# A first ternary product from bfloat16 parts, joined matmul runs, and some of a scan's weighted sums on GpSimd

## The chip, the core and the metric

The kernel runs on one core of a Trainium2 chip. The core has a matrix engine (TensorE, PE in the profile, with its weight loads shown as PEld), a vector engine (VectorE, DVE), a scalar engine for activation functions and copies (ScalarE, ACT), a general engine (GpSimd, POOL) and a queue for transfers (SyncE, SP). Operands lie in SBUF, 128 partitions wide; matmuls write to PSUM, which has eight banks of 128 x 512 float32. GpSimd's instructions here all work in SBUF. The metric is the device time of one launch, in microseconds (us), the median of several runs.

## The reference

The model takes 128 batches of 32 tokens with 256 features (4096 rows in all) and sends them through six residual layers in two levels. Cut to what matters:

```
x = x + cross_attention_0(ctx, layernorm(x))          # softmax over 257 context rows, weights wq, wk, wv
x = x + selective_scan(layernorm(x))                  # 512 channels, 16 states, along the 32 tokens
x = x + ternary_mlp(x)                                # 256 -> 1024 -> 256
x = x + focused_linear_attention(layernorm(x), ctx)   # 16 heads
x = x + latent_attention(layernorm(x))                # 16 heads, keys and values through 64 latents
x = x + quantized_mlp(x)                              # 8-bit rows, ternary weights
```

Two of them are touched by the change:

```
# selective scan: gate, x and delta are projections; A = -exp(A_log), c0 = C_mat[0]
def step(h, (x_t, d_t)):
    h = h * exp(A * d_t[..., None]) + (x_t * d_t)[..., None] * B_mat      # 512 x 16
    y_t = h @ c0                                                          # sum over the 16 states
y = y + x * D_vec;  out = (gate * y) @ W_out.T + b_out

# ternary mlp: absmean(W) = sign(W / g) * min(round(|W / g|), 1), with g = mean |W| + 1e-6
h = x @ absmean(W_fc).T
h = layernorm(gelu(h), ln_w, ln_b)
out = h @ absmean(W_proj).T
```

The ternary weights are -1, 0 and 1. The mlp's input is normalised too: the kernel computes each row's mean and reciprocal deviation, takes the mean off the input or off the weights, and multiplies the deviation in as the scale of the gelu.

## The kernel before

Rows are worked on in 32 groups of 128 (four batches of 32 tokens), and the groups in nine blocks of 2, 4, 4, 4, 4, 4, 4, 4 and 2. For each block there are three stages:

- **Context (`c`)**: `context_group` does the first cross attention of one group and, from the same context rows, the keys and values of the later linear attention (`keys`, `keys_values`). Its float32 matmuls `pkey` and `pval` are the largest part of TensorE's work.
- **Scan (`a`)**: `scan_block` works on a whole block at once, 512 columns (256 in the first and the last block). There are four channel blocks of 128 channels, and each has 16 states. For each state ScalarE computes the decay `a`, DVE scans along the tokens (`tensor_tensor_scan`, giving `h`) and DVE adds `h` times the state's weight `w_st` to `acc`, which lies in a bank of PSUM. `acc` begins as the projection `xd` times `d_vec`, written by ScalarE. After the last state `acc` is multiplied by the gate.
- **Layers (`l`)**: `latent_group` does the four other layers of one group: `mlp`, `linear`, `attention` and `quantized_mlp`, and stores the rows.

In `mlp` the rows of x are transposed as they are, while two statistics run beside this; two runs of two float32 matmuls each (k = 0 and 1, 512 columns each) multiply by `w_fc`, from whose rows the mean was taken off in the set-up (`centred(w_fc, 2)`). In `attention` four runs of matmuls follow one another: the query `pqa`, the latents `plat`, the keys `pka` and, further on, the values `pva`, each in a PSUM bank of its own, with ScalarE's copies between them.

No engine is given its instructions in the order of the program. Every call goes through a `Recorder` (so nearly every instruction in the profile has one line, L540), and a planner, `order`, then places them. It has a cost for each instruction (`ns_of`, with `TAIL` and `HOP` for what passes before another engine can go on), a pair of due times for every group of instructions (`DUE`, one pair for each call of `begin`), and a few settings: `PRICE` weighs the engines where an instruction may go to more than one (`copy`, `relu`, `scaled`), `WINDOW` and `SOONER` let a more urgent instruction go first, and `HORIZON` says how far ahead of the front a new buffer may be opened. Matmuls under one `R.together()` are placed as one run, back to back. The order found is fixed on each engine; what waits is then only for data and buffers. Buffers come from rings: `t2` has 15 tiles of 2 KB per partition, `bank` the eight PSUM banks, and `a_ring` three tiles for the decays.

Of the kernel before, what the change touches and what calls it, by code (L numbers as in the profile page):

```python
# [16 lines left out]
P = 128  # L17
# [77 lines left out]
TAIL = {"vector": 75, "scalar": 100, "gpsimd": 25, "tensor": 130, "sync": 0}  # L95
# [171 lines left out]
class Recorder:  # L267
# [8 lines left out]
    def together(self):  # L276

        recorder = self

        class Joined:  # L280
            def __enter__(self):
                recorder.joined = []

            def __exit__(self, *_):
                parts, recorder.joined = recorder.joined, None
                ways = {"tensor": ([c for p in parts for c in p[0]], sum(p[1] for p in parts), False)}
                recorder.add(ways, [r for p in parts for r in p[2]], [w for p in parts for w in p[3]])

        return Joined()

    def copy(self, out, in_):
        self.record({"scalar": ("copy", (out, in_), {}), "vector": ("tensor_copy", (out, in_), {})})

# [12 lines left out]
    def begin(self, stage):  # L306

        self.stage = stage
        self.group += 1
        self.spans[self.group] = DUE[self.group]  # L310

    def record(self, calls):
# [33 lines left out]
        if self.joined is not None:  # L346
            self.joined.append((*ways["tensor"][:2], reads, writes))
            return
# [205 lines left out]
PRICE = {"tensor": 0.0, "vector": 3.195, "scalar": 3.454, "gpsimd": 8.58, "sync": 0.0}  # L554
WINDOW = 31.919
SOONER = -0.015
AHEAD = 0
HORIZON = 0.832
# [3 lines left out]
def perceiver_kernel(ctx: ExitStack, tc: tile.TileContext, t: dict, out: bass.AP):  # L562
# [92 lines left out]
    def t2k(shape, name, dtype=F32):  # L655
        return ring("t2", 15).tile(shape, name, dtype)
# [51 lines left out]
    w_fc = wts.tile([P, 2, HID], F32, name="w_fc")  # L708
# [135 lines left out]
    def late_setup():  # L844
# [52 lines left out]
        centred(w_fc, 2)  # L897
# [142 lines left out]


# [73 lines left out]
    def scan_block(x):  # L1115
        size = len(x)
        tok, batches = size * P, size * GB
# [17 lines left out]
        for ic in range(4):  # L1135

            dl = t2k([P, TOK], "dl")[:, 0:tok]
            R.scalar.activation(
                dl, project(w_in, DI + ic * P), AF.Relu, bias=b_in[:, 4 + ic : 5 + ic]
            )  # L1140
            xd = project(w_in, ic * P)
            acc = bank("acc")[:, 0:tok]
            R.scalar.activation(
                acc, xd, AF.Identity, bias=bd_in[:, ic : ic + 1], scale=d_vec[:, ic : ic + 1]
            )
            R.vector.scalar_tensor_tensor(xd, xd, b_in[:, ic : ic + 1], dl, ALU.add, ALU.mult)
            dv = dl.rearrange("p (b q) -> p b q", q=LQ)
            for s in range(NST):

                a = a_ring[s % NA][:, 0:batches, :]  # L1150
                R.scalar.activation(
                    a[:, :, 1:LQ], dv[:, :, 1:LQ], AF.Exp, scale=a_neg[:, ic, s : s + 1]
                )
                h = t2k([P, TOK], "h")[:, 0:tok]
                R.vector.tensor_tensor_scan(
                    h, a.rearrange("p b q -> p (b q)"), xd, 0.0, ALU.mult, ALU.add
                )
                R.vector.scalar_tensor_tensor(
                    acc, h, w_st[:, ic, s : s + 1], acc, ALU.mult, ALU.add
                )  # L1160
            R.vector.tensor_tensor(yg[ic], acc, yg[ic], ALU.mult)
        for g in range(size):
# [8 lines left out]
    def mlp(xg):  # L1171

        _, r = stats(xg)
        xT = rows_T(xg)
# [3 lines left out]
        for k in range(2):  # L1178
            ph = bank("ph")
            cols = slice(k * 512, (k + 1) * 512)  # L1180
            with R.together():
                accumulate(ph, [(xT[:, dc, :], w_fc[:, dc, cols]) for dc in range(2)])
# [64 lines left out]
    def attention(xg):  # L1247
# [3 lines left out]
        with R.together():  # L1251
            for c in range(2):
# [3 lines left out]
                )  # L1256
        qT = t1k([P, D], "qTa").rearrange("p (c n) -> p c n", c=2)
        R.scalar.copy(qT, pq[:, 0:D].rearrange("p (c n) -> p c n", c=2))

        pl_ = bank("plat")  # L1260
        with R.together():
            accumulate(pl_[0:LAT, 0:P], [(wkd[:, dc], xT[:, dc, :]) for dc in range(2)])
        lat = t1k([P, P], "lat")[0:LAT]
        R.scalar.copy(lat, pl_[0:LAT, 0:P])

        pk = bank("pka")
        with R.together():
            for c in range(2):
                accumulate(pk[:, c * P : (c + 1) * P], [(wupk[:, c * P : (c + 1) * P], lat)])
        kd = t2k([P, 2, GB, 2, LQ], "kd")  # L1270
        for r in range(2):
# [3 lines left out]
                scale=odd[:, r : r + 1],  # L1275
            )
# [25 lines left out]

        vd = vds[turn[0] % NV]
        turn[0] += 1
        pv = bank("pva")
        with R.together():
            for b in range(GB):
                for r in range(4):
                    R.tensor.matmul(
                        pv[r * LQ : (r + 1) * LQ, b * 64 : (b + 1) * 64],  # L1310
                        lat[:, b * LQ : (b + 1) * LQ],
                        wupv.rearrange("p (j h k) -> p h j k", h=4, k=16)[:, r],
                        start=True, stop=True,
                    )
        for r in range(4):
            rows_ = slice(r * LQ, (r + 1) * LQ)
            R.scalar.copy(
                vd[rows_, :, :, r, 0:16],
                pv[rows_, 0 : GB * 64].rearrange("p (b j n) -> p b j n", b=GB, j=4),
            )  # L1320
# [88 lines left out]
    def latent_group(xg, kvc, rows_out):  # L1409
        mlp(xg)  # L1410
        linear(xg, kvc)
        attention(xg)
        quantized_mlp(xg)
# [4 lines left out]
    for i, size in enumerate(BLOCKS):  # L1418
# [12 lines left out]
        scan_block(x)  # L1431
# [8 lines left out]
NV = 2  # L1440
PAIR = 2
# [4 lines left out]
    (-1.0, -0.9), (-0.011, 0.566), (-0.809, -0.789), (-0.212, 0.821), (-0.767, 0.109),  # L1446
    (-0.01, 0.15), (0.299, 1.222), (0.556, 1.717), (1.591, 2.698), (1.87, 3.034), (0.619, 0.719),
    (0.863, 0.989), (1.148, 1.233), (1.17, 1.732), (1.498, 2.663), (2.591, 3.75425),
    (2.699, 3.86225), (2.806, 3.97), (2.915, 4.07825), (1.618, 1.802), (1.854, 2.163),
    (2.11, 2.23), (2.365, 2.485), (2.459, 3.663), (3.593, 4.75425), (3.7, 4.86225),  # L1450
    (3.807, 4.97025), (3.915, 5.07825), (2.571, 2.704), (2.985, 3.032), (3.115, 3.236),
    (3.365, 3.485), (3.5, 4.663), (4.591, 5.75425), (4.699, 5.86225), (4.807, 5.97025),
    (4.915, 6.07825), (3.61, 3.735), (3.864, 3.99), (4.115, 4.235), (4.365, 4.431), (4.5, 5.663),
    (5.591, 6.755), (5.699, 6.86225), (5.807, 6.97025), (5.915, 7.113), (4.615, 4.733),
    (4.866, 5.033), (5.115, 5.235), (5.365, 5.485), (5.5, 6.663), (6.612, 7.776), (6.72, 7.884),
    (6.7, 8.26), (6.921, 8.145), (5.616, 5.733), (5.924, 6.173), (6.117, 6.235), (6.462, 6.482),
    (6.501, 7.654), (7.288, 8.301), (7.441, 8.497), (7.544, 8.812), (7.594, 8.984),
    (6.632, 6.743), (6.921, 6.941), (7.171, 7.295), (7.361, 7.611), (7.495, 8.077),
    (7.815, 9.377), (7.667, 9.18), (7.008, 8.283), (7.34, 8.982), (7.658, 7.783), (7.829, 7.849),
    (8.0, 8.585), (8.023, 9.464), (8.392, 9.052),  # L1460
# [78 lines left out]
```

## Time and profile before

| | |
|---|---|
| median of 3 runs | 1763.43 us (1761.84 to 1765.21) |
| the profiled execution | 1760.93 us |
| its span, first to last instruction | 1759.2 us |
| TensorE (PE) busy | 1660.5 us, 94% |
| VectorE (DVE) busy | 1554.4 us, 88% |
| ScalarE (ACT) busy | 1430.8 us, 81% |
| GpSimd (POOL) busy | 1117.0 us, 63% |
| mean granted TensorE clock | 0.973 of full speed |
| transfers | 59.69 MB, 34 GB/s on average |

A group of instructions is shown as engine, operation, result and operands, shape and count, then the busy time in us and the mean duration of one in ns, and last the time for which the engine was idle just before them and what ended that. A float32 matmul appears as two records. Matmuls overlap in the array, so the mean duration of one is more than what it adds to a row of them; some records of matmuls are missing from the trace. In a line by stretch of time the first figures are the stretch and its length, then the busy time and number of instructions of each engine, the granted clock and the load of the transfers.

### The profile page before, as it was taken

Reading aid. Unit: us, or ns where it says so; the run is one execution under the profiler, and the core shown is the slowest. Engines: PE = TensorE matmul, PEld = TensorE weight load, DVE = VectorE, ACT = ScalarE, POOL = GpSimd, SP = SyncE. Lnnn points to the kernel's source line nnn. Section 1 sums busy time; section 2 is a strip of 40 time slices with the busy share of each in tenths; the row PEclk is TensorE's granted clock in tenths of the full one; section 3 lists DMA queues with packets and bytes.
Section 4 is the critical chain, followed back from the end, with each engine's and each line's share of the span. In section 5 each row is a group of like instructions: output and inputs, shape, how many; then the busy total and the mean of one; then the engine's idle time right before and its main releaser. Section 6 shows DMA issues by size and latency. Waiting matters only on the chain.

```text
span 1759.2 us, 44923 instructions
## 1 busy us (share of the span) xinstructions
PE 1660.5 (94%) x17268; PEld 1211.7 (69%) x17299; DVE 1554.4 (88%) x3083; ACT 1430.8 (81%) x3442; POOL 1117.0 (63%) x1827
## 2 busy tenths in 40 slices
PE   8999999999999999999999999999999989597886
PEld 6787667766776777766776767766776667366564
DVE  3599799999898999899899999979999999999865
ACT  4587888888788997889788888889888898786655
POOL 5675556744776677666776747865776375347476
PEclk9999999999999999999999999999999999798886
DMA  7221101000110011001100021001100000000000
GB/s 243 74 83 47 61 29 32 29 31 4 48 42 2 16 59 35 29 2 40 41 29 29 7 65 37 29 2 40 40 29 29 1 8 20 4 4 5 5 4 22
DMA packets 44758, 59.69 MB, mean 34 GB/s; under 512 B 8704, under 2 KB 27008, under 8 KB 44544
## 3 DMA queue, kind: packets, MB, share of 16 engines
q1 hardware_dynamic: 44544, 56.81, 10.1%
q8 instruction: 137, 2.24, 0.5%
q14 instruction: 77, 0.63, 0.1%
HBM read 52.32 MB, written 4.19 MB: 32 GB/s over the span
## 4 chain that ended last, share of the span: by engine, by line
PE 75%; DVE 12%; ACT 7%; issue 1%; POOL 1%; DMA 0%; SPq 0%; DVEq 0%; ACTq 0%; POOLq 0%
PE pkey L540 13%; PE pval L540 11%; PE pproj L540 9%; PE pT L540 5%; PE pmlp L540 5%; DVE h L540 5%; PE ph L540 4%; PE pk L540 3%; PE pcT L540 3%; PE pout L540 3%; PE pq L540 3%; DVE acc L540 2%; PE psc L540 2%; PE pqa L540 2%; PE po L540 2%; PE pya L540 2%
## 5 line engine op out<-in xcount | busy, mean ns | idle before, releaser
L540 DVE TENSOR_TENSOR_SCAN h<-a,pproj 128x512 f32<-128x512 f32 (+1 forms) x576 | 617.4, 1087 | 12.4 <-ACT a L540 11.6
L540 ACT ACTIVATE a<-dl,a_neg 128x496 f32<-128x496 f32 (+1 forms) x576 | 369.8, 662 | 60.9 <-DVE h L540 57.6
L540 DVE SCALAR_TENSOR_TENSOR acc<-h,w_st,acc 128x512 f32<-128x512 f32 (+1 forms) x576 | 392.4, 681 | 0.1
L540 PE MATMUL pval<-wkv,cT 128*128 128x256 f32 x1024 | 245.7, 385 | 8.8 <-ACT hid L540 2.3
L540 PE MATMUL pkey<-wkv,cT 128*128 128x256 f32 x1024 | 238.1, 386 | 0.0
L540 POOL TENSOR_TENSOR ku<-ku,e 128x512 f32<-128x512 f32 x128 | 162.1, 1276 | 101.1 <-ACT ku L540 93.3
L540 PEld LDWEIGHTS pval<-wkv,cT 128*128 128x128 f32 x1024 | 189.6, 191 | 44.6 <-issue 7.4
L540 ACT ACTIVATE ks<-ku 128x256 f32<-128x256 f32 x512 | 208.1, 412 | 14.3 <-POOL ku L540 13.1
L540 PEld LDWEIGHTS pkey<-wkv,cT 128*128 128x128 f32 x1024 | 189.3, 190 | 37.7 <-issue 14.5
L540 POOL TENSOR_TENSOR ku<-ks,ku 128x512 f32<-128x512 f32 x128 | 163.7, 1285 | 29.8 <-ACT ks L540 29.1
L540 ACT ACT_TABLE_LOAD x114 | 146.3, 1283 | 5.1 <-PE ph L540 2.5
L540 POOL TENSOR_TENSOR kn<-kn,halves 128x4 f32<-128x4 f32 x128 | 134.1, 1048 | 22.5 <-ACT ks L540 21.7
L540 ACT ACTIVATE vf<-pval,kf 128x256 f32<-128x256 f32 x256 | 107.9, 471 | 40.0 <-PE pval L540 24.5
L540 POOL TENSOR_TENSOR rstd<-rstd,halves 128x1 f32<-128x1 f32 x224 | 123.7, 553 | 15.8
L540 POOL TENSOR_SCALAR rstd<-mv 128x1 f32<-128x1 f32 x224 | 42.9, 192 | 133.7 <-DVE mv L540 110.2
L540 PE MATMUL pproj<-xTs,w_in 128*128 128x512 f32 (+1 forms) x288 | 122.4, 552 | 0.5 <-ACT hT L540 0.2
L540 PE MATMUL ph<-w_fc,xT 128*128 128x512 f32 x256 | 120.2, 597 | 0.6 <-ACT xT L540 0.5
L540 PE MATMUL pmlp<-w_pr,hT 128*128 128x256 f32 x512 | 116.7, 381 | 1.5 <-ACT hT L540 1.2
L540 PEld LDWEIGHTS pmlp<-w_pr,hT 128*128 128x128 f32 x512 | 95.8, 190 | 20.7 <-issue 4.8
L540 ACT ACTIVATION_READ_ACCUMULATOR ks<-ku 128x1 f32 x512 | 99.4, 194 | 0.0
L540 ACT COPY cT<-pcT 128x512 f32<-128x512 f32 x128 | 71.8, 595 | 12.2 <-PE pcT L540 11.8
L540 DVE BATCH_NORM_STATS2 st<-x 128x6 f32<-128x256 f32 x192 | 78.7, 413 | 2.9 <-POOL x L540 1.7
(259 smaller groups left out, 3583.1 us busy)
## 6 DMA issues: line engine op xcount, KB each, us to landing
cx<-in_ctx_dram SPq DMA_DIRECT2D x64, 512.0 KB
x<-in_x_dram SPq DMA_DIRECT2D x32, 128.0 KB
cr<-in_ctx_dram SPq DMA_DIRECT2D x128, 32.0 KB
out_dram<-x SPq DMA_DIRECT2D x32, 128.0 KB
vlz<-vl SPq DMA_DIRECT2D x128, 1.1 KB
w_in<-in_w_inT_dram SPq DMA_DIRECT2D x1, 1024.0 KB
raw_fc<-in_w_fcT_dram SPq DMA_DIRECT2D x2, 512.0 KB
raw_pr<-in_w_prT_dram SPq DMA_DIRECT2D x2, 512.0 KB
```

What stands on the lines that cost most here:

```text
L540: ins = getattr(engine, name)(*(traced(a) for a in args), **{k: traced(v) for k, v in kw.items()}).ins
```

## The change

- In `mlp` the mean is now taken off x before the transposition, not off `w_fc`. The transposed rows are split into three bfloat16 parts (a cast, what is left, a cast, what is left), and the run for each half has six bfloat16 matmuls in place of two float32 ones. `w_fc` is stored in bfloat16, which holds -1, 0 and 1 exactly. The casts may go to three engines (`cast`), the subtractions to two (`either`).
- In `attention` the latents are computed in the run of the query, and the values in the run of the keys, in one bank each; the copies into `vd` come before the scores.
- In `scan_block` the first two states (the first four in the last two blocks) are weighted and summed by GpSimd in a tile `some` in SBUF, which starts as the projection times `d_vec`. DVE's first weighting then adds to `some` and writes `acc`, whose bank is opened only there.
- The planner gets other costs, prices and settings; a run is charged 15 or 90 ns more; `t2` has 17 tiles; `part` divides the stages (the contexts in two, the scan by channel block, the layers by layer), so that `DUE` has 251 pairs in place of 78.

```diff
-TAIL = {"vector": 75, "scalar": 100, "gpsimd": 25, "tensor": 130, "sync": 0}
+TAIL = {"vector": 75, "scalar": 90, "gpsimd": 25, "tensor": 215, "sync": 0}
...
+                small = any(p[4] for p in parts)
+                ns = sum(p[1] for p in parts) + (90 if small else 15)
+                ways = {"tensor": ([c for p in parts for c in p[0]], ns, False)}
...
+    def cast(self, out, in_):
+        self.record({
+            "scalar": ("copy", (out, in_), {}), "vector": ("tensor_copy", (out, in_), {}),
+            "gpsimd": ("tensor_copy", (out, in_), {}),
+        })
...
+    def part(self):
         self.group += 1
         self.spans[self.group] = DUE[self.group]
...
-PRICE = {"tensor": 0.0, "vector": 3.195, "scalar": 3.454, "gpsimd": 8.58, "sync": 0.0}
-WINDOW = 31.919
-SOONER = -0.015
-AHEAD = 0
-HORIZON = 0.832
+PRICE = {"tensor": 0.0, "vector": 2.435, "scalar": 0.756, "gpsimd": 0.394, "sync": 0.0}
+WINDOW = 39.422
+SOONER = 0.032
+AHEAD = 0.074
+HORIZON = 1.395
...
-        return ring("t2", 15).tile(shape, name, dtype)
+        return ring("t2", 17).tile(shape, name, dtype)
...
-    w_fc = wts.tile([P, 2, HID], F32, name="w_fc")
+    w_fc = wts.tile([P, 2, HID], BF16, name="w_fc")
...
-        centred(w_fc, 2)
...
+        pooled = LATE_POOLED if late else POOLED
...
-            acc = bank("acc")[:, 0:tok]
+            some = t2k([P, TOK], "some")[:, 0:tok]
             R.scalar.activation(
-                acc, xd, AF.Identity, bias=bd_in[:, ic : ic + 1], scale=d_vec[:, ic : ic + 1]
+                some, xd, AF.Identity, bias=bd_in[:, ic : ic + 1], scale=d_vec[:, ic : ic + 1]
             )
...
-                R.vector.scalar_tensor_tensor(
-                    acc, h, w_st[:, ic, s : s + 1], acc, ALU.mult, ALU.add
-                )
+                weight = w_st[:, ic, s : s + 1]
+                if s < pooled:
+                    R.gpsimd.tensor_scalar(h, h, weight, None, ALU.mult)
+                    R.gpsimd.tensor_tensor(some, some, h, ALU.add)
+                else:
+                    if s == pooled:
+                        acc = bank("acc")[:, 0:tok]
+                    R.vector.scalar_tensor_tensor(
+                        acc, h, weight, some if s == pooled else acc, ALU.mult, ALU.add
+                    )
...
     def mlp(xg):
-
-        _, r = stats(xg)
-        xT = rows_T(xg)
+        mv, r = stats(xg)
+        xc = t1k([P, D], "xc")
+        R.either.tensor_scalar(xc, xg, mv[:, 0:1], None, ALU.subtract)
+        xT = t1k([P, D], "xT")
+        transposed(xc, xT.rearrange("p (c n) -> p c n", c=2), 2)
+
+        x3 = t2k([P, 3, D], "x3", BF16)
+        R.cast(x3[:, 0, :], xT)
+        R.either.tensor_tensor(xT, xT, x3[:, 0, :], ALU.subtract)
+        R.cast(x3[:, 1, :], xT)
+        R.either.tensor_tensor(x3[:, 2, :], xT, x3[:, 1, :], ALU.subtract)
...
-                accumulate(ph, [(xT[:, dc, :], w_fc[:, dc, cols]) for dc in range(2)])
+                accumulate(ph, [
+                    (x3[:, k3, dc * P : (dc + 1) * P], w_fc[:, dc, cols])
+                    for dc in range(2) for k3 in range(3)
+                ])
...
+            accumulate(pq[0:LAT, D : D + P], [(wkd[:, dc], xT[:, dc, :]) for dc in range(2)])
+        lat = t1k([P, P], "lat")[0:LAT]
+        R.scalar.copy(lat, pq[0:LAT, D : D + P])
...
         pk = bank("pka")
+        pv = pk[:, D : 2 * D]
         with R.together():
             for c in range(2):
                 accumulate(pk[:, c * P : (c + 1) * P], [(wupk[:, c * P : (c + 1) * P], lat)])
+            for b in range(GB):
+                for r in range(4):
+                    R.tensor.matmul(
+                        pv[r * LQ : (r + 1) * LQ, b * 64 : (b + 1) * 64],
+                        lat[:, b * LQ : (b + 1) * LQ],
+                        wupv.rearrange("p (j h k) -> p h j k", h=4, k=16)[:, r],
+                        start=True, stop=True,
+                    )
...
-        scan_block(x)
+        scan_block(x, i >= len(BLOCKS) - 2)
...
+POOLED = 2
+LATE_POOLED = 4
```

## The prediction

> **What bounds the kernel now.** The execution that was profiled took 1760.9 us, 1.7 us more than its span of 1759.2 us and 2.5 us less than the median of the runs, 1763.4 us. I sum against the span and add 4.2 us at the end. First I read the busy times by stretch. The cuts are mine: set-up up to 200 us, the regular blocks up to 1400, then up to 1661, where the last scan and its weighting end, and the rest.
>
> ```profile
> core 0: us, PE busy (x) PEld busy (x) DVE busy (x) ACT busy (x) POOL busy (x), PEclk, DMA share, GB/s
> 0.00:200.00 200.00, 188.93 (x1810) 146.19 (x1811) 143.57 (x330) 135.35 (x419) 128.29 (x206) 0.98 0.33 105
> 200.00:1400.00 1200.00, 1177.13 (x12356) 855.34 (x12377) 1102.88 (x2044) 1035.18 (x2475) 781.39 (x1265) 1.00 0.09 30
> 1400.00:1560.00 160.00, 132.11 (x1274) 95.87 (x1276) 155.46 (x290) 131.46 (x284) 81.78 (x142) 0.94 0.03 10
> 1560.00:1661.00 101.00, 86.02 (x1104) 61.94 (x1104) 90.87 (x243) 75.58 (x168) 56.18 (x92) 0.88 0.02 4
> 1661.00:1759.00 98.00, 76.34 (x729) 52.34 (x732) 61.64 (x179) 53.20 (x99) 69.35 (x124) 0.78 0.04 12
> ```
>
> From 200 to 1400 TensorE (PE) is busy 98% and VectorE (DVE) 92%: matmul time decides. From 1400 to 1661 the context matmuls run out (the last `pval` is at 1484 us), PE falls to 84%, and DVE is busy 246.3 of 261 us: the scans of the last two blocks decide. In the last 98 us nothing is full: that is the latency of the last groups' layers, one operation after the other. GpSimd (POOL) has room everywhere. Then the groups of instructions that the change touches, or that are nearest to what it adds:
>
> ```profile
> L540 PE MATMUL ph<-w_fc,xT 128*128 128x512 f32 x256 | 120.2, 597 | 0.6 <-ACT xT L540 0.5 <-DVE hq L540 0.2
> L540 DVE SCALAR_TENSOR_TENSOR acc<-h,w_st,acc 128x512 f32<-128x512 f32 x448 | 332.1, 741 | 0.1
> L540 DVE SCALAR_TENSOR_TENSOR acc<-h,w_st,acc 128x256 f32<-128x256 f32 x128 | 60.5, 472 | 0.0
> L540 POOL TENSOR_TENSOR ku<-ks,ku 128x512 f32<-128x512 f32 x128 | 163.7, 1285 | 29.8 <-ACT ks L540 29.1
> L540 POOL TENSOR_SCALAR hq<-hq,qm 128x1024 f32<-128x1024 f32 x32 | 35.7, 1115 | 14.6 <-DVE qm L540 13.7
> L540 POOL TENSOR_SCALAR q<-xn 128x256 bf16<-128x256 f32 x32 | 12.9, 403 | 34.6 <-DVE xn L540 29.3 <-DVE qm L540 4.3
> L540 POOL TENSOR_TENSOR x<-x,s 128x256 f32<-128x256 f32 x32 | 23.3, 728 | 13.6 <-PE pT L540 9.3 <-DVE st L540 4.2
> ```
>
> The reader sees that a weighting on DVE costs 0.741 us (0.472 for the small blocks), and an addition on POOL 1.28 us (0.73). Mean durations of matmuls overlap, so for them I take starts from the timeline:
>
> ```profile
> 1567.62 1.88 PE L540 MATMUL ph<-w_fc,xT 128*128 128x512 f32 x4
> 1569.34 3.62 PE L540 MATMUL pmlp<-w_pr,hT 128*128 128x256 f32 x16
> ...
> 1685.53 1.03 PE L540 MATMUL phq<-w,qT 128*128 128x512 bf16 x4
> 1686.40 0.38 PE L540 MATMUL pT<-ident,x 128*128 128x128 f32 x2
> ```
>
> A float32 run of `ph` (two products, four records) holds PE for 1.72 us; four bfloat16 products of the same width hold it for 0.87, so 0.2175 each, with a new stationary tile for each.
>
> **The change, part by part.** *The product itself.* A run becomes six bfloat16 matmuls: 6 x 0.2175 = 1.305 us, a gain of 0.415 a run, 26.6 us over 64 runs. Of the 256 records 199 lie between 200 and 1400 us (about 50 runs, 20.6 us), 43 up to 1661 and 16 after it. Only the first 20.6 us shorten a stretch that PE sets; the rest falls where PE has idle time.
>
> *The centring of `w_fc` in the set-up goes.* Two runs like the old `ph`, 3.4 us of PE, and some 3.9 us of DVE. PE is busy 94% of that stretch: 3 us.
>
> *The new work per group* is a centring of x and four operations that split it (cast, rest, cast, rest), on 256 columns. On POOL: 0.47 (403 ns plus one pointer, about 70 ns) + 2 x 0.40 + 2 x 0.73 = 2.73 us, 87 us over 32 groups; on DVE about 0.41 + 2 x 0.35 + 2 x 0.415 = 1.94 us, 62 us. The new prices make POOL and ScalarE (ACT) cheaper against DVE than before, so I give DVE a third, 21 us. ACT, at 81%, can take the casts at 0.37 us. None of it binds before 1661, as POOL and ACT have room and DVE loses more than it gains. In the last stretch it is latency: the transposes now wait for the statistics too (0.42 + 0.18 us) and then for 0.44 + 2 x 0.39 + 2 x 0.57, so 3.0 us with hops left out, less a little on PE: +3 us (0 where the other group of the last block covers it, +6 where both groups pay in series).
>
> *Joined runs.* Four runs per group become two in the first half of attention: `lat` with `q`, `v` with `k`. In the timeline eight records of `pqa` hold PE 0.98 us, or 0.245 a product, and the two products of `plat` 0.58, so a run's edge costs at most 0.09 us: 64 edges, 0 to 5.8 us. The waits before `plat` and `pva` are 1.7 and 1.6 us in all. I take 3 us of 0 to 9. The queue behind a joined run waits longer for its first result, by 0.6 us, which later matmuls of other groups cover.
>
> *The pooled states.* Full width: 6 blocks x 4 channel blocks x 2 states, and 16 in the late block: 64 weightings x 0.741 = 47.4 us less on DVE. Half width: 8 in the first block and 16 in the last, 24 x 0.472 = 11.3. Together 58.7 us, 19.4 of it in the two late blocks, whose scans lie almost wholly between 1400 and 1661. POOL pays a multiplication (between the 256- and 1024-wide rows, 0.62 plus 0.07 for the pointer: 0.69 us) and an addition (1.28): 1.97 us x 64 + 1.20 x 24 = 155 us. At most 1117 + 155 + 87 = 1359 us, 80% of the span: still not the bound. DVE goes to about 1554 - 59 - 4 + 21 = 1512. In the stretch from 1400 to 1661, which DVE sets, I count 19.4 less some 4 for splits: -15 us (bounds -8 with all splits on DVE, -19 with none).
>
> *The shared port.* The trace shows DVE held up by POOL now and then: `xn` takes 405 ns in the median and 1439 at worst. The scans, with one operand in PSUM, run at 1165 to 1221 ns beside a POOL that is two thirds busy:
>
> ```profile
> L540 DVE TENSOR_TENSOR_SCAN h<-a,pproj x71: 1165/1210/1221, 300.4 to 498.5; 128x512 f32<-128x512 f32 x71
> ```
>
> Only 36 of the weightings (the first after the pooled states, which now reads `some` and `h` from SBUF) join the exposed kind; at the mean excess of `xn`, 34 ns, that is 1 us, at its worst 37 us. I take 1, as most DVE time keeps an operand in PSUM.
>
> The Trainium skill speaks against this part: "Perfetto Trace Analysis", section "Optimizing Scalar/DVE Operations", says that GpSimd and DVE share an SBUF read port, so that moving work between those two might not help. By the rule the 15 us of the late stretch would be nothing and the sum 15 us higher. The row of the scans above disagrees with it for operations that read PSUM, and I go by the row.
>
> *The order.* Every priority in the planner changes: 251 due spans in place of 78, so each layer and channel block gets its own, two more `t2` buffers, two PSUM banks fewer per attention, `acc` opened two states later, a longer horizon. No row prices this. The bounds: PE idles 66 us between 200 and 1661 (23 + 28 + 15); all of it saved would be -66, twice as much idle +66. Nearest is the stretch to 1400: DVE has 97 us idle there, and 39 more once 58.7 - 19.4 us of weightings are gone, while the late stretch is full of DVE work. Scans of the last blocks brought forward into a seventh of that room of 136 us give -20. I take -20, towards a gain because in both long stretches one engine is near full while another has room.
>
> **Sum.** 1759.2 - 20.6 - 3 - 3 - 15 + 3 + 1 - 20 = 1701.6; with 4.2 us, 1706 us.
>
> **The rivals.** *Smaller gain: the order brings nothing.* Without its -20 the time is 1726. For it: PE is 98% busy to 1400, and the last 98 us are latency that no order shortens. Against it: 136 us of DVE room before 1400. *Larger gain:* the order uses half of the 66 us of PE idle and a third of DVE's room, -50 in place of -20: 1676. For it: the last stretch, where DVE has 36 us free and PE 22, could take work of the groups before, so that the last scan ends sooner. Against it: such work must be ready, and the end stays a chain. *Slower: DVE waits for POOL.* In each channel block the first weighting on DVE waits for all pooled additions. Uncovered, that is 3.9 us for two states less the 1.2 of the second scan, and a POOL queue in order, whose head may wait too:
>
> ```profile
> POOL rstd L540 <- DVE mv L540: 110.2, 57, 11.4
> POOL ku L540 <- ACT ku L540: 93.3, 36, 13.7
> ```
>
> The second is 2.6 us a time. So 5.3 us in 28 channel blocks, and 7.9 - 3.6 + 2.6 = 6.9 in the 8 late ones: 204 us. DVE's idle time between 200 and 1661 is 112 us, and 59 come free; past 171 us, or 4.75 us per channel block, the kernel is slower, here by 33: about 1796. Behind the waiting weighting stand all of DVE's other work and the bank of `acc`. Against it: the planner puts other scans and layers between (the timeline has scans in pairs ahead of their weightings), and 17 buffers hold the h tiles. *No change:* the gains are eaten by port waits at their worst (37 us) and an order that loses some 20.
>
> **How the numbers follow.** Forecast (1690 to 1720) 0.42, smaller gain (1720 to 1745) 0.25, larger gain (1660 to 1690) 0.22, slower 0.08, no change 0.03. The prediction is 1706 us; 1668 to 1740 leaves out about 2 in 10 and takes in the bounds of all parts but the order's. Runs differ by about 0.2% from one another, so that much is "same": faster 0.89, same 0.03, slower 0.08.
>
> **What would show it.** PE busy near 1627 us (1660.5 - 26.6 - 3.4 - 3); `ph` runs of six matmuls in 1.3 us; 488 DVE weightings in place of 576; POOL near 1300 us; DVE and PE both well over 90% up to the last scan, which ends before 1620 us; some 100 us behind it. It is wrong if DVE idles before weightings that wait for `some`, if `ph` holds PE over 1.5 us a run, or if PE's idle time grows.

## The result: 1.3% slower, and the profile after

The changed kernel takes 1785.51 us in the median of 4 runs (1783.40 to 1786.25), the kernel before 1762.63 us beside it (1759.63 to 1765.21): a ratio of 1.0128, with an interval of 1.0109 to 1.0148. The forecast was 1706 us, faster, with a range of 1668 to 1740. The sign is wrong, and the time is 79.5 us over the forecast. It is not the clock of TensorE: the mean granted clock of the profiled execution is 0.972, and it was 0.973 before.

The busy times of the changed kernel by stretch, with the columns as before; the last cut is again the end of the last scan's weighting, which lies at 1677.9 us here and lay at 1661:

```profile
core 0: us, PE busy (x) PEld busy (x) DVE busy (x) ACT busy (x) POOL busy (x), PEclk, DMA share, GB/s
0.00:200.00 200.00, 186.26 (x1854) 146.13 (x1855) 137.15 (x316) 140.10 (x438) 146.22 (x227) 1.00 0.34 106
200.00:1400.00 1200.00, 1151.93 (x12315) 836.99 (x12350) 1054.89 (x1943) 1016.35 (x2455) 974.73 (x1438) 0.99 0.09 29
1400.00:1677.90 277.90, 230.90 (x2181) 164.10 (x2193) 247.25 (x504) 216.50 (x464) 225.52 (x325) 0.91 0.02 7
1677.90:1784.50 106.60, 81.73 (x1018) 57.53 (x1022) 70.21 (x209) 66.87 (x128) 83.83 (x149) 0.88 0.03 11
```

In the stretch to 1400 us, PE was busy 1177 of 1200 us before and is busy 1152 now. That alone could be right, as the bfloat16 product takes less time; but the program isn't ahead at 1400 us: the rest of it lasts 384.5 us, where it lasted 359.2. POOL has gone from 65% to 81% of that stretch. The groups that answer to those shown of before:

```profile
L553 DVE SCALAR_TENSOR_TENSOR acc<-h,w_st,acc 128x512 f32<-128x512 f32 x356 | 263.3, 740 | 0.4
...
L553 POOL TENSOR_TENSOR ku<-ks,ku 128x512 f32<-128x512 f32 x128 | 163.7, 1286 | 16.1 <-ACT ks L553 15.2
...
L553 POOL TENSOR_SCALAR h<-h,w_st 128x512 f32<-128x512 f32 x64 | 100.4, 1570 | 40.1 <-DVE h L553 34.6 <-DVE qm L553 2.0 <-DVE mv L553 1.7
...
L553 PE MATMUL ph<-w_fc,x 128*128 128x512 bf16 x356 | 91.8, 384 | 11.5 <-POOL x L553 6.4 <-DVE x L553 1.6 <-ACT hid L553 0.8
...
L553 POOL TENSOR_TENSOR some<-some,h 128x512 f32<-128x512 f32 x64 | 81.4, 1271 | 4.5
...
L553 POOL TENSOR_SCALAR hq<-hq,qm 128x1024 f32<-128x1024 f32 x32 | 36.4, 1138 | 6.1 <-PE po L553 3.7 <-DVE mv L553 1.1
...
L553 POOL TENSOR_SCALAR xc<-x,mv 128x256 f32<-128x256 f32 x32 | 30.5, 954 | 0.5
...
L553 DVE SCALAR_TENSOR_TENSOR acc<-h,w_st,some 128x512 f32<-128x512 f32 x28 | 29.5, 1054 | 9.9 <-POOL some L553 9.6
...
L553 POOL TENSOR_SCALAR h<-h,w_st 128x256 f32<-128x256 f32 x24 | 22.5, 938 | 13.3 <-DVE h L553 8.4 <-ACT a L553 4.9
```

Two prices stand out. POOL's weighting `h<-h,w_st` takes 1.570 us at 512 columns and 0.938 at 256, where the prediction had 0.69 and less; the centring `xc` 0.954, where it had 0.47. Yet `hq<-hq,qm`, also a multiplication by a pointer, but with an addition behind it, does 1024 columns in 1.138 us (1.115 before). The addition has its forecast price (1.271, forecast 1.28), and `ku` its price of before. DVE's first weighting after the pooled states, with both operands in SBUF, takes 1.054 us in place of 0.740.

The product itself does what was forecast. In PE's timeline two runs of `ph` in a row (twelve matmuls, one record missing) begin at 403.27, and the next work begins 2.59 us later, 1.295 us a run (forecast 1.305):

```profile
403.27 2.75 PE L553 MATMUL ph<-w_fc,x 128*128 128x512 bf16 x11
405.86 0.60 PE L553 MATMUL pT<-ident,hid 128*128 128x128 f32 x4
```

The chain that ended last, by engine, of the kernel before:

```profile
PE 75%; DVE 12%; ACT 7%; issue 1%; POOL 1%; DMA 0%; SPq 0%; DVEq 0%; ACTq 0%; POOLq 0%
```

Then the same line of the changed kernel, in which POOL has a quarter:

```profile
PE 41%; POOL 25%; DVE 19%; ACT 10%; issue 5%; DMA 0%; POOLq 0%; SPq 0%; DVEq 0%; ACTq 0%
```

And, of the changed kernel, waits by the engine that waits and what it waits for (total us, number, longest): POOL's own two that were shown of before, and the longest waits of other engines for POOL. The two for `some`, the sums of the pooled states, are among them, but they are not the large ones:

```profile
POOL rstd L553 <- DVE mv L553: 41.3, 24, 7.3
...
POOL ku L553 <- ACT ku L553: 31.6, 18, 9.7
ACT ks L553 <- POOL ku L553: 27.2, 43, 3.9
...
DVE xn L553 <- POOL rstd L553: 17.2, 8, 8.4
PEld L553 <- POOL q L553: 16.0, 13, 4.7
PEld pk L553 <- POOL vf L553: 15.5, 29, 2.0
...
PEld pT L553 <- POOL xc L553: 12.6, 12, 3.5
...
PE pqT L553 <- POOL q L553: 10.9, 10, 4.2
...
DVE h L553 <- POOL some L553: 10.3, 6, 4.8
DVE acc L553 <- POOL some L553: 10.2, 8, 2.1
```

POOL itself waits for `mv` for 41 us in place of 110, as it has other work. All waits of other engines for POOL in this list (rows of 1 us and more in total) come to 221 us, against 88 us before; the waits of PE's loads and of PE itself are both counted, so this sum is no measure of the time lost. The order on POOL is fixed by the planner, so `rstd`, `q`, `ku` and `vf`, which the change doesn't touch, come later when a 1.57 us weighting stands ahead of them.

### The profile page after: what moved, and what is told of

It reads as the page before. It is cut to its first block, busy times and chain, and to the rows that moved or that the text cites. A ratio compares the mean times of both kernels' runs of the same rounds, so it can differ in the third digit from the quotient of the medians.

```text
span 1784.5 us, 45393 instructions
## 1 busy us (share of the span) xinstructions
PE 1650.8 (93%) x17365; PEld 1204.8 (68%) x17419; DVE 1509.5 (85%) x2970; ACT 1439.8 (81%) x3484; POOL 1430.3 (80%) x2136
## 4 chain that ended last, share of the span: by engine, by line
PE 41%; POOL 25%; DVE 19%; ACT 10%; issue 5%; DMA 0%; POOLq 0%; SPq 0%; DVEq 0%; ACTq 0%
DVE h L553 8%; PE pkey L553 7%; PE pval L553 6%; DVE acc L553 5%; PE pproj L553 5%; POOL h L553 4%; POOL ku L553 4%; POOL some L553 3%; PE pT L553 3%; POOL rstd L553 3%; PE pmlp L553 3%; PE pqa L553 2%; PE pcT L553 2%; PE pk L553 2%; POOL x L553 2%
## 5 line engine op out<-in xcount | busy, mean ns | idle before, releaser
L553 DVE SCALAR_TENSOR_TENSOR acc<-h,w_st,acc 128x512 f32<-128x512 f32 (+1 forms) x452 | 308.7, 683 | 0.6
L553 PE MATMUL pkey<-wkv,cT 128*128 128x256 f32 x1024 | 242.6, 391 | 0.0
L553 POOL TENSOR_SCALAR h<-h,w_st 128x512 f32<-128x512 f32 (+1 forms) x88 | 122.9, 1397 | 53.4 <-DVE h L553 43.0
L553 PE MATMUL pmlp<-w_pr,hT 128*128 128x256 f32 x512 | 120.7, 390 | 0.9 <-ACT hT L553 0.8
L553 PEld LDWEIGHTS pmlp<-w_pr,hT 128*128 128x128 f32 x512 | 98.2, 196 | 16.3 <-ACT hT L553 1.1
L553 POOL TENSOR_TENSOR some<-some,h 128x512 f32<-128x512 f32 (+1 forms) x88 | 100.6, 1143 | 6.1
L553 PE MATMUL ph<-w_fc,x 128*128 128x512 bf16 x356 | 91.8, 384 | 11.5 <-POOL x L553 6.4
```

The source lines that it names most:

```text
L553: ins = getattr(engine, name)(*(traced(a) for a in args), **{k: traced(v) for k, v in kw.items()}).ins
```

## The experiments

Three things could be behind the 79.5 us: the prices on POOL, some other cost of the work that POOL was given (waits for the sums, the shared port, the latency of the split), or the order that the planner makes. The runs go in this manner: first a price is changed with the order of every engine held still, then work is left out with the order held still, then the order is changed with the work held still. Where the text says that the order is the same, the traces have the same sequence of instructions on DVE, ACT, POOL and in PE's weight loads, but for what is left out or moved. Ratios are to the kernel before on the same chip (1764.34 to 1765.61 us); the runs come from several chips, so the ratios decide where a difference is small.

### Prices, at the order of the changed kernel

**Both with a second operation.** The weighting and the centring get a second operation that multiplies by 1.0.

```diff
-R.gpsimd.tensor_scalar(h, h, weight, None, ALU.mult)
+R.gpsimd.tensor_scalar(h, h, weight, 1.0, ALU.mult, ALU.mult)
...
-R.either.tensor_scalar(xc, xg, mv[:, 0:1], None, ALU.subtract)
+R.either.tensor_scalar(xc, xg, mv[:, 0:1], 1.0, ALU.subtract, ALU.mult)
```

> GpSimd's multiplication of h by the state's weight and the centring of x get a second operation that changes nothing (times 1.0); the order of all engines stays as in the changed kernel. Theory A, the form of the instruction: with one operation it takes 1.57 us (512 columns) and 0.95 us (256), with two it takes what the two-operation rows suggest, about 0.69 and 0.47 us; 82 us of GpSimd time go and the time falls to 1690 to 1725 us. Theory B, the order made by the new due times is bad in itself: at least 1770 us. Theory C, handing the sums to GpSimd costs waits and port time whatever the form: 1745 to 1775 us.

Measured: 1752.34 us, 0.9916 (0.9888 to 0.9944): 0.8% faster than before, by an operation more. The price of the weighting is theory A's, but the time is not: it lies in theory C's range, 27 us over A's. The groups of this run:

```profile
L553 POOL TENSOR_SCALAR h<-h,w_st 128x512 f32<-128x512 f32 x64 | 44.3, 693 | 44.7 <-DVE h L553 37.4 <-DVE qm L553 2.6 <-DVE mv L553 1.7
...
L553 POOL TENSOR_SCALAR xc<-x,mv 128x256 f32<-128x256 f32 x32 | 37.0, 1157 | 2.4
...
L553 DVE SCALAR_TENSOR_TENSOR acc<-h,w_st,some 128x512 f32<-128x512 f32 x28 | 24.2, 864 | 0.9 <-POOL some L553 0.5 <-ACT eT L553 0.3
...
L553 POOL TENSOR_SCALAR h<-h,w_st 128x256 f32<-128x256 f32 x24 | 11.4, 478 | 14.0 <-DVE h L553 8.4 <-ACT a L553 5.0
```

The weighting falls from 1.570 to 0.693 us and from 0.938 to 0.478: 0.84 ns a column in place of 2.47, by the two widths, with a start of some 0.3 us in both forms. So 0.69 was the price of another form of the same product. The centring becomes slower, 1.157 us. And DVE's first weighting, `acc<-h,w_st,some`, falls from 1.054 to 0.864 us though nothing of it was changed, and DVE's idle time before it from 9.9 to 0.9 us.

**The weighting alone**, with the centring as in the change.

> Only the weighting of h on GpSimd gets the second operation; the centring keeps its one (0.95 us, where the two-operation form with a subtraction took 1.16). Same order as in the changed kernel. If GpSimd's own time is what is lost, the time follows it: some 1745 us, a little under the run in which both were changed (1752). If the weighting alone was the harm and the centring is hidden, 1750 to 1754 us.

Measured: 1750.84 us, 0.9922 (0.9903 to 0.9941). The weighting's form is worth 34.7 us (1785.51 - 1750.84; by the ratios 36). Of the two expectations it is the second, with a centring whose extra 0.2 us is hidden: by the ratios this run isn't faster than the one before. The waits for POOL fall from 221 to 141 us.

**The weighting, and a centring that multiplies first**: x times -1 plus the mean, with the signs of `w_fc` turned in the set-up.

```diff
...
-R.either.tensor_scalar(xc, xg, mv[:, 0:1], None, ALU.subtract)
+R.either.tensor_scalar(xc, xg, -1.0, mv[:, 0:1], ALU.mult, ALU.add)
```

> Weighting with two operations, and the centring as x times -1 plus the mean (a multiplication first), with the signs of the first ternary weights turned, so that the product is the same. Same order. The multiplication-first form should take about 0.47 us in place of 1.16: 22 us less of GpSimd, which stands before TensorE's transposes. Theory A (GpSimd's queue late against the order): 1725 to 1742 us. Theory B (what remains is the order itself): 1748 us or more.

Measured: 1743.05 us, 0.9873 (0.9851 to 0.9896), another 7.8 us on the same chip. It is 1 us over theory A's range and under B's, so it decides neither. The row of the centring:

```profile
L553 POOL TENSOR_SCALAR xc<-x,mv 128x256 f32<-128x256 f32 x32 | 16.0, 500 | 2.6
```

This version, of 1743.05 us, is the base of several runs below. Its stretches up to the end of the last scan's weighting:

```profile
core 0: us, PE busy (x) PEld busy (x) DVE busy (x) ACT busy (x) POOL busy (x), PEclk, DMA share, GB/s
...
200.00:1400.00 1200.00, 1167.58 (x12484) 853.35 (x12522) 1080.94 (x1991) 1040.41 (x2495) 942.62 (x1478) 0.99 0.09 29
1400.00:1633.80 233.80, 198.71 (x2012) 142.41 (x2019) 215.44 (x456) 187.93 (x420) 177.71 (x283) 0.93 0.03 8
```

**The centring on DVE**, at its place in the order, with the quick weighting.

> Weighting with two operations, and the centring moved from GpSimd to VectorE at its place in the order: 32 x about 0.42 us there, 37 us less on GpSimd. Theory A: 1725 to 1742 us, like the fast form. If VectorE is the one that is late: 1755 us or more.

Measured: 1742.68 us, 0.9875 (0.9848 to 0.9902), the same gain; the operation takes 0.405 us on DVE. So it was the length of the one-operation form that cost. Whether it cost as time of POOL or as delay ahead of the transposes isn't shown, as both runs shorten both. With both prices right, the change is 1.3% faster than the kernel before, and still 37 us over the forecast.

### Work left out, at the same order

**The sums.** The 88 weightings and 88 additions on POOL are not emitted; the output lacks the first 2 states, in the last two blocks the first 4. The rest is as in the first experiment.

> Both operations of the centring and weighting in the two-operation form, and the 88 weightings and 88 additions on GpSimd are left out of the program, the rest in the same order: the first 2 (late 4) states are missing from the scan's sum. GpSimd falls by some 155 us to about 1215 us. Theory A and theory C (port, waits for the sums): 1700 to 1720 us, TensorE idle in the stretch from 200 to 1400 us under 25 us. Theory B: above 1735 us, since nothing but the order is left.

Measured: 1743.30 us, 0.9885 (0.9858 to 0.9912). It is in theory B's range, and PE is idle for 36 us to 1400 us, not under 25. It is 9.0 us under its counterpart of 1752.34, which ran on another chip; by the ratios 5.5, with intervals that overlap. At their forecast price the sums, their waits and the port together cost 5 to 9 us, hardly clear of the scatter; the prediction had 1, for the port.

**The split**, from the version of 1743.05 us: one of its four operations is kept, and all six products read that part.

> The version with the two-operation weighting and the quick centring (1743.05 us), same order on every engine, but of the four operations that split x into three parts only the first cast is kept; the six products of ph all read the first part, so the product has one part three times instead of x. TensorE's work is the same. Theory (the order is what is left): the split costs only the latency at the end that was forecast with +3, so 1733 to 1741. Rival (the split's latency, 1.9 to 3 us before each of 32 layers, is what keeps TensorE idle): 1710 to 1728, with the idle time of TensorE between 200 and 1400 us back near 23 us from 32.

Measured: 1740.48 us, 0.9864 (0.9843 to 0.9885), 2.6 us less, within the scatter of the two and in the theory's range. The latency of the split isn't what holds the kernel up.

**The split and the sums.** POOL has 1143.5 us of work left, 26 us more than before the change.

> As the run before, and the 88 weightings and 88 additions on GpSimd are left out too (the output lacks the first 2, in the last two blocks 4, of the 16 states), so GpSimd has less than 1150 us of work and nothing new waits for it but the centring; same order on every engine. Theory (the order): 1722 to 1735, still 15 us or more above the forecast 1706. Rival (what GpSimd was given costs the missing 37 us in some way that neither part shows alone): 1700 to 1712.

Measured: 1737.47 us, 0.9841 (0.9820 to 0.9863), a little over the expected 1722 to 1735 and far from the rival's 1700 to 1712. By stretch:

```profile
core 0: us, PE busy (x) PEld busy (x) DVE busy (x) ACT busy (x) POOL busy (x), PEclk, DMA share, GB/s
...
200.00:1400.00 1200.00, 1172.81 (x12548) 855.82 (x12547) 1079.54 (x1997) 1046.82 (x2509) 802.67 (x1307) 0.99 0.09 30
1400.00:1628.50 228.50, 196.69 (x2004) 141.87 (x2002) 211.28 (x451) 183.60 (x412) 131.12 (x215) 0.91 0.03 8
1628.50:1737.00 108.50, 83.07 (x1020) 58.44 (x1020) 70.27 (x209) 66.89 (x128) 79.89 (x143) 0.87 0.03 11
```

Against the run before, on the same chip, the sums are worth 3.0 us, within the scatter. With a POOL nearly as lightly loaded as before, PE still has 27 us of idle time to 1400 us (23 before the change), and the stretch behind the last scan still takes 108.5 us (98.2 before). 31 us of the distance to the forecast are in neither the price nor the amount of POOL's new work.

### The order

**No pooled states**, with all else of the change and its due times.

```diff
-POOLED = 2
-LATE_POOLED = 4
+POOLED = 0
+LATE_POOLED = 0
```

> The changed kernel with no state on GpSimd (0 and 0 in place of 2 and 4); the centring keeps its one operation. GpSimd falls by some 224 us to about 1205 us, VectorE rises by 59 to about 1560 us. Theory A: about 1735 us, GpSimd being free again and VectorE back where it was. Theory B: at least 1775 us. Theory C: 1705 to 1730 us, better than the two-operation run.

Measured: 1990.70 us, 1.1264 (1.1234 to 1.1295). Work is taken from POOL and given back to DVE, 59 us of it by the prediction's rows, and the time grows by 205. This is theory B's range. It fits that due times serve only the instructions that they were made for, but doesn't show it, as the planner made a new order here.

**Pooled states alone**, put into the kernel before, with its due times. (No run has the new product alone.)

> The kernel before, with its own due times and prices, and only the pooled states added (2 and 4, one operation as in the change). Theory A: GpSimd rises to about 1340 us, of which some 67 us are not in the planner's costs, 1765 to 1790 us. Theory B: the old order gains from the pooled states, 1735 to 1755 us. Theory C: slower than before, 1775 us or more, as DVE's first weighting waits for the sums.

Measured: 1865.72 us, 1.0556 (1.0528 to 1.0584). Its weighting on POOL took 1.568 us, so the price goes with the form and not with this order; the time is in theory C's range, but the run can't separate price, waits and order.

**The right price for the planner.** The changed kernel's own instructions, with the one-operation form costed at 320 ns plus 2.43 a column; the order differs, and with it the engine of some instructions.

```diff
             pointers = sum(is_ap(kw.get(k)) for k in ("scalar1", "scalar2"))
+            if kw.get("scalar2") is None:
+                return 320 + 2.43 * n
```

> The changed kernel, where the planner's cost of a one-operation GpSimd instruction is set to what the trace shows (320 ns + 2.43 ns a column); the instructions stay as they are, the order differs. Theory A with the wrong price as its main harm (engines wait where the order expected GpSimd to be done): 1720 to 1750 us. Theory A with GpSimd's own time as its main harm: 1760 to 1785 us. Theory B: at least 1775 us.

Measured: 1879.08 us, 1.0630 (1.0597 to 1.0664): 94 us slower than the changed kernel with the same instructions, of which POOL has 26 fewer (2110 for 2136) and DVE 28 more; only theory B allows this time. A truer cost made a worse order; that the due times, which stayed, are the reason is likely but not shown.

**One setting back**, from the version of 1743.05 us: the horizon, then the window.

```diff
-HORIZON = 1.395
+HORIZON = 0.832
```

> The version of 1743.05 us, nothing left out, with one setting of the planner as before the change (horizon 0.832 in place of 1.395): the same instructions in another order. Theory (the order decides by tens of us, and due times and settings belong together): more than 10 us away from 1743 with GpSimd's and VectorE's busy times within 2% of it; most likely slower, 1755 to 1850. Rival (the order is worth little, the engines' work sets the time): 1736 to 1750.

Measured: 1939.86 us, 1.0987 (1.0962 to 1.1013).

```profile
core 0: us, PE busy (x) PEld busy (x) DVE busy (x) ACT busy (x) POOL busy (x), PEclk, DMA share, GB/s
...
200.00:1400.00 1200.00, 1096.10 (x11042) 782.49 (x11041) 967.14 (x1763) 941.00 (x2248) 842.88 (x1320) 0.94 0.09 27
1400.00:1824.00 424.00, 352.85 (x3555) 250.74 (x3552) 349.91 (x706) 313.45 (x699) 289.40 (x456) 0.90 0.04 11
```

PE's idle time to 1400 us is 104 us with the same instructions (32 in the version of 1743.05), and the granted clock there is 0.94 in place of 0.99. DVE's busy time in all is 1520.7 us (1503.4), within the 2%; the time is 90 us over the most likely range.

```diff
-WINDOW = 39.422
+WINDOW = 31.919
```

> As the run before, with the planner's window as before the change (31.919 in place of 39.422) and the horizon as after it. Theory (the order): more than 10 us away from 1743, either way, at the same busy times; where the time goes shows as TensorE's idle time between 200 and 1400 us (32 us at 1743) or in the stretch behind the last scan. Rival: 1736 to 1750.

Measured: 1856.64 us, 1.0520 (1.0488 to 1.0552). The theory's direction was open, and both came out slower. So far the order was only shown to be able to lose time; for the forecast's missing gain it had to be shown to win some.

**A third order.** The due times and settings were searched anew, by random steps, for a sooner planned end; the instructions are those of the version of 1743.05 us. Against that version the whole edit is numbers: these and the 251 pairs of `DUE`. With them the planner also puts five instructions on another engine (four `ku` on DVE and one cast on POOL in place of ACT).

```diff
-PRICE = {"tensor": 0.0, "vector": 2.435, "scalar": 0.756, "gpsimd": 0.394, "sync": 0.0}
-WINDOW = 39.422
+PRICE = {"tensor": 0.0, "vector": 1.453, "scalar": 0.46, "gpsimd": 0.073, "sync": 0.0}
+WINDOW = 39.948
 SOONER = 0.032
-AHEAD = 0.074
-HORIZON = 1.395
+AHEAD = 0.026
+HORIZON = 1.413
...
```

> The instructions of the version of 1743.05 us, nothing left out, in a third order: new due times and settings of the planner, found by a search for a sooner planned end (23.1 us sooner by the planner's own costs than the order of the change; no instruction is added or taken away). Three orders of the same instructions ended 29, 39 and 53 us after their planned ends, the sooner ones closer. Theory (the forecast's missing gain is the order's): 1713 to 1728, at GpSimd's, VectorE's and ScalarE's busy times within 2%, with the last scan ending before 1620 us or TensorE's idle time in all under 95 us (106.9 at 1743). Rival (something else that the change adds holds the time up, so a better plan doesn't come through): 1736 to 1750.

Measured: 1717.86 us in the median of 5 runs (1717.78 to 1719.33), 0.9729 (0.9707 to 0.9752). It is the fastest version of the study, 2.7% faster than the kernel before and 3.8% faster than the changed one. Its busy times in all:

```profile
PE 1626.9 (95%) x17365; PEld 1197.9 (70%) x17419; DVE 1501.3 (87%) x2974; ACT 1430.3 (83%) x3476; POOL 1352.0 (79%) x2137
```

Its scans, with the start of the first and the last of them behind the three durations:

```profile
L553 DVE TENSOR_TENSOR_SCAN h<-a,pproj x576: 626/1205/1225, 105.5 to 1607.5; 128x512 f32<-128x512 f32 x149, 128x256 f32<-128x256 f32 x43
```

And its stretches:

```profile
core 0: us, PE busy (x) PEld busy (x) DVE busy (x) ACT busy (x) POOL busy (x), PEclk, DMA share, GB/s
...
200.00:1400.00 1200.00, 1179.54 (x12617) 861.81 (x12656) 1099.23 (x2025) 1061.66 (x2552) 967.59 (x1513) 1.00 0.10 30
1400.00:1610.00 210.00, 179.16 (x1913) 131.51 (x1920) 193.22 (x419) 169.51 (x378) 160.59 (x256) 0.93 0.03 8
1610.00:1717.50 107.50, 84.42 (x1036) 59.90 (x1042) 72.24 (x215) 64.96 (x127) 84.12 (x150) 0.88 0.04 11
```

PE is idle for 20 us to 1400 us, and the last scan begins at 1607.5 us, where it began at 1676.5 in the changed kernel and at 1632.4 in the version of 1743.05. The stretch behind it takes 107.5 us as in the others. The kernel before was not given such a new search, so it isn't shown how much of the 25 us by which this order beats the version of 1743.05 is room that the change made, and how much such a search would have won there too.

**Another search**, stopped at a planned end that is 10.4 us sooner than the change's, not 23.1.

> As the run before, with the due times of another search, whose planned end is 10.4 us sooner than that of the change's order. Theory: between the two, 1727 to 1738. Rival: 1736 to 1750, with no relation to the plan.

Measured: 1734.35 us, 0.9817 (0.9790 to 0.9844), between the two as expected.

**The third order with the slow weighting** of the change.

> The third order, with the weighting on GpSimd in the change's own form of one operation (1.57 us at 512 columns in place of 0.69). Theory: the form's price holds in another order too, 20 to 45 us over the run before the last. Rival (the 34 us between the change and its repaired form belonged to that one order): under 15 us.

Measured: 1757.83 us, 0.9949 (0.9932 to 0.9966): 40.0 us over 1717.86. The form's price isn't a property of one order: 34.7 us in the one, 40.0 in the other. The weighting's row in the third order, and in this run:

```profile
L553 POOL TENSOR_SCALAR h<-h,w_st 128x512 f32<-128x512 f32 x64 | 44.2, 691 | 34.1 <-DVE h L553 26.7 <-PE pk L553 2.7 <-DVE sm L553 2.7
...
L553 POOL TENSOR_SCALAR h<-h,w_st 128x512 f32<-128x512 f32 x64 | 100.4, 1570 | 25.0 <-DVE h L553 20.3 <-PE pk L553 2.8 <-DVE sm L553 1.4
```

## Why the prediction was wrong

**The account.** 1785.51 - 34.7 (form of the weighting) - 7.8 (form of the centring) - 25.2 (third order in place of the change's) = 1717.9, and 11.9 us to 1706 stay. All three are differences between runs in which one thing was changed; by the ratios they are 36, 9 and 25.

**The step that failed first: the price of the multiplication on POOL**, "between the 256- and 1024-wide rows, 0.62 plus 0.07 for the pointer: 0.69 us". The two rows were of another form: both have two operations (`q<-xn` adds a constant and multiplies by 1.0, with a bfloat16 result and no pointer; `hq<-hq,qm` multiplies by a pointer and adds a constant). In the kernel before, every `tensor_scalar` on GpSimd has two operations, and two of them, `q` and `rstd`, have a multiplication by 1.0 that changes nothing. The form that the change issues, one operation with a pointer, was in no row of before, and a form that isn't in the trace should have had bounds far apart. It measured 1.57.

**What hung on it: "POOL ... at most 1359 us, 80% of the span: still not the bound".** On this the sum gave POOL's new time no term. POOL reached 1430 us and 80% of a longer span. That it wasn't full says little: what counts is what stands in its queue behind the new work. In the changed kernel 25% of the chain that ended last is on POOL, in the version of 1743.05 us 6%, and the waits for POOL fall from 221 to 123 us. The rival "DVE waits for POOL" had the right engine and the wrong waiters: the two waits of DVE for `some` were 20.5 us in all, far under its 171. The larger waits are those of PE, ACT and DVE for `rstd`, `q`, `ku`, `vf` and `xc`, which the rival didn't count. No rival had a higher price for the operation. So a short way to a slower time, one unmeasured price, was left out of the chance of 0.08 for a slower kernel.

**The centring**, 0.47 forecast, 0.954 measured: the same mistake, worth 7.8 us. The first experiment shows that a second operation isn't enough: with one behind the subtraction it rose to 1.157. Of the three forms of the centring on POOL only the product ahead of an addition gave 0.50; yet `q<-xn`, an addition ahead of a product, but with constants, takes 0.403, so no simple rule follows.

**The order, -20.** This was a guess between -66 and +66, and the text said that no row prices it. In the order that the change came with, the gain didn't come: with POOL's new work left out the time was 1737.5, over the 1726 of the sum without the order's term. A third order won 25 us over it. So there was room, as the prediction read from the stretches (PE's 66 us idle between 200 and 1661), but it takes due times that fit, and whether the change came with such could not be seen in the profile of before. That 25 us are near the 20 is luck: no row priced them, and they came from a search that the forecast didn't know of. A planned order is part of a change, and its term can be larger than all others together: 1718 to 1940 us with the same work.

**The port, +1.** The group of 28 weightings with two operands in SBUF cost 8.8 us more than 28 at 0.740 in the changed kernel, 314 ns each where the prediction took 34, and 3.5 us more, 124 ns each, with the short weighting. The Trainium skill, "SBUF — State Buffer", section "Who interferes with whom", says that a DVE instruction with two operands in SBUF contends with a GpSimd instruction that reads SBUF, and that the shared ports are an exclusive lock. The rows fit this: same order, same DVE instruction, 1.054 us beside weightings of 1.57, 0.864 beside weightings of 0.69 and 0.796 where the sums are left out; most single ones stay near 0.75, and those over 0.9 us are 15, 9 and 5 of 36 (both widths). The rule that was weighed in the prediction, that moving work between these two engines might not help, would have made the late stretch's -15 nothing. At the change's order the stretch from 1400 us to the end of the last scan went from 261 us to 277.9 with the slow form, and to 233.8 in the version of 1743.05. That is shorter than before, against the rule, but part of it is work done earlier or later, and no run has the weightings back on DVE in an order made for that; so whether the move as such helps isn't shown.

**The end, +3.** The stretch behind the last scan went from 98.2 to 106.6 us in the changed kernel and 107.5 in the third order, +8 to +9. Leaving out the split didn't shorten it (108.5), so it isn't the split. What the traces show is more work there: PE has 1018 to 1036 instructions in it for 729 before, and the query matmuls `pqa` of the latent attention, 8 records a group, are 32 in place of 16. So the attention of two more groups lies behind the last scan in the new orders. That this lengthens the stretch is likely, but no run tests it. The 6 us over the forecast's +3 are about half of the 11.9 us that are left; the rest stays open.

**Right:** the product (1.295 us a run for 1.305), DVE's 488 weightings, and, in the third order, PE's busy time (1626.9 for 1627; 1650.8 in the changed kernel) and the last scan before 1620 us. DVE's busy time (1509.5 for 1512) is right in part by luck: the splits, put at 21 us on DVE, all ran on POOL and ACT, and 14.4 us of `ku` left DVE for ACT, while the weightings fell by 48.7 us for 58.7, and `xn` rose from 41.2 to 50.0 us. The signs that the prediction named did their work: "if PE's idle time grows" is what happened (98.7 to 133.7 us). The gain of the joined runs, 3 us, wasn't taken apart.

## What to carry to other kernels

Price an instruction by its whole form (how many operations, which comes first, pointer or constant, types), and when the trace has no row of that form, let its bounds be a factor of two or three apart and make one of the rivals out of it. When work goes to an engine that has room, ask what stands behind it in that engine's queue and who waits for that, not only who waits for the new result. And where an order was planned for given instructions, a change of instructions, of a cost or of a setting without a new search of its due times says little about the change: hold the order still to learn a price, and search again before judging the change.

## What the runs showed of the hardware

- On GpSimd, a float32 `tensor_scalar` with one operation and a pointer takes 2.47 ns a column (1.570 us at 512, 0.938 at 256); with a second operation, multiplication by 1.0, it takes 0.84 (0.693 and 0.478). An operation more made it 2.3 times as fast at 512 columns. Why isn't shown.
- With the subtraction of a pointer first, 256 columns take 0.954 us alone and 1.157 us with a multiplication behind it; a multiplication by a constant with the addition of a pointer behind it takes 0.500. Whether the subtraction or the place of the pointer makes the difference isn't shown.
- The Trainium skill, "GPSIMD Engine Reference", section "4.1 Engine selection", has elementwise work with one input at roughly line rate on GpSimd. The short form fits that better than the long one: DVE does the product and an addition of 512 columns in 0.740 us, and the one-operation product alone takes 1.570 on GpSimd, so for that form the measurement speaks against the rule.
